# The last feed-forward part of two tiles held back, joined to 256 tokens and placed in the last tile's chain

## The chip, the core and the metric

The kernel runs on one core of one Trainium2 chip. A core has five instruction queues that run side by side: PE (TensorE, matmuls into PSUM; its weight loads are listed as PEld), DVE (VectorE), ACT (ScalarE), POOL (GpSimd) and SP (SyncE, which here issues nearly all DMAs). The metric is the device time of one execution in microseconds (us), as the median of several runs. One further execution was taken by the hardware profiler, and all views quoted here are of that one.

## The reference

Three layers are applied to 16 sequences of 64 tokens, 1024 tokens of 256 numbers in all. Each layer is added to its input after a layer norm.

```python
x = x + xattn(layernorm(x), ctx_2048, ...)   # self- and cross-attention, 16 heads over 1601 context rows per sequence
x = x + attn(layernorm(x), ...)              # block attention and a gated feed-forward with ternary weights
x = x + ffn(layernorm(x), ...)               # the part that this change moves

def ffn(x, gate_w, up_w, down_w, gate_s, up_s, down_s):
    g = einsum('th,ih->ti', x, gate_w) * gate_s      # 256 -> 704
    u = einsum('th,ih->ti', x, up_w) * up_s          # 256 -> 704
    return einsum('ti,hi->th', silu(g) * u, down_w) * down_s   # 704 -> 256
```

Nearly all work is in the cross-attention of the first layer. Everything is in float32 or rounded to coarser grids inside it.

## The kernel before

The 1024 tokens are eight tiles of 128 tokens (two sequences each). The tiles are counted from 0 in the code (`i`), so the sixth, seventh and last tile are `i` = 5, 6 and 7.

**Units.** For each tile there are two halves of the heads (`hh`) and two sequences (`bb`), so four units, and each unit goes through 13 chunks of up to 128 context rows (`unit`, L465). A chunk is projected to keys (L488, `ps_k`), squared and normalised (L493 to L507), transposed (L521, `tr_kx`), scored (L534, `s`), and 18 to 20 steps later, when the maximum over all chunks is known, exponentiated (L585 on DVE, L589 on ACT) and summed with the context rows into three PSUM accumulators (L604, `acc`). The context rows for the last step are loaded by L481 into five rotating buffers `ctxN`.

**After a unit.** The sums are divided (L613 to L618, `pq`), transposed (`turn_contexts`, L627, `tr_pc`) and, once per half, multiplied by the value weights and the output weights (`pair_out`, L647: `po_x` at L661, rounding on DVE at L673 and L192 to L265, `po_p` at L278, added to the tile's row `xr[i]` at L282). For the last half of the last tile `gap` is `None`, and both groups are done without a pause between them.

**Last parts.** `last_parts` (L782) then does layers two and three for one tile of 128 tokens. It is one long chain: a norm, the quantised projection (L774 transposes `tr_aq`, L792 `ps_qk`, L797 `ps_v`), the rotation (`r1`, `r2`), the transposes `tr_qk` (L821), four quarters of small attention, the output projection `po_o` (L885, added at L886), a norm ending in `hn` (L752), `tr_hn` (L893), the first feed-forward (L900 `ps_g`, `ps_u`; L909 `po_d`), and then the part that the change moves: the norm `xn3`, its transpose (L922), six chunks of 128 or 96 inner features (L938, four matmuls into `pgu`; Silu on ACT at L943; the product on DVE at L944), and `po_f` (L956, six matmuls), scaled and added on DVE (L961, L962) and stored (L963).

**What sets the order.** Every piece of work is a generator with a step and a rank on a heap (`spawn`, `at`, `run`, L83 to L100): a lower step goes first, then a lower rank, and `yield n` puts the rest n steps later. A tile takes 52 steps. `last_parts` of tile `i` starts at step 52*i + 92; for the seventh tile at +80 and for the last at +74 (L997). A scheduling layer below that then moves instructions of an engine past each other when the program is built, with the written order as priority, and puts in all waits. After that each engine's order is fixed.

**Buffers.** Weights for all of this come by DMA into one pool `wp` of ten buffers (L65, `piece` at L200). The DMAs stand in SP's queue in a fixed order, and one that waits for a buffer holds those behind it. `s_tile` and `tr_tile` take one of three PSUM banks, `ps_mm` has two more, used for `ps_k`. The pool `pp` (19 buffers) holds the exponentiated chunks.

The lines that the steps below use:

```python
        l0 = base + {NT - 2: 80, NT - 1: 74}.get(i, 92)
        spawn(l0, 2.5, last_parts(i, l0))
```

Of the kernel before, what the change touches and what calls it, by code (L numbers as in the profile page):

```python
# [14 lines left out]
F32 = mybir.dt.float32  # L15
# [8 lines left out]
P = 128  # L24
# [34 lines left out]
def body(tc, ctx, a):  # L59
# [586 lines left out]

    def pair_out(i, hh, gap):  # L647
# [28 lines left out]
        if gap is None:  # L676
            ws = [w_p, weights("wproj", 5 + 2 * hh)]
            pos = [group(gp) for gp in range(2)]
            for gp in range(2):
                project_out(i, rounded(gp, pos[gp]), ws[gp])  # L680
            return
# [56 lines left out]
    def b2(name):  # L738
        return one.tile([P, 512], F32, tag="b2", name=name, bufs=3)
# [42 lines left out]
    def last_parts(i, start):  # L782
# [3 lines left out]
        norm_apply(xa, xr[i], st, 1, H)  # L786
        h = yield from rmsnorm(xa, rows[:, 0, :], "h")
# [16 lines left out]
        q4 = qk.rearrange("p (h e d) -> p h e d", h=32, e=2)  # L804
        r1, r2 = b2("r1"), b2("r2")
# [80 lines left out]
        V.scalar_tensor_tensor(xa, po[:, 0:H], f, xa, ALU.mult, ALU.add)  # L886
        w_up = [piece("wup", (lambda t: t, cols_of("ffn_up_w", 0, 1024)[:, k, :])) for k in range(2)]
# [20 lines left out]
        for k in range(4):  # L908
# [18 lines left out]
        for c, (c0, n) in enumerate(CHUNKS):  # L927
            if c == 3:
                w_gu = [
                    piece("w_ff", (lambda t: v2(t[:, 0:640]), cols_of(name, 384, 320))) for name in ("gate_w", "up_w")  # L930
                ]
                yield 2
            c1 = c0 if c < 3 else c0 - 384
            pgu = s_tile("pgu")
            for e in range(2):
                w = v2(w_gu[e][:, 0 : 768 if c < 3 else 640])
                for k in range(2):
                    PE.matmul(  # L938
                        pgu[:n, e * P : (e + 1) * P], lhsT=w[:, k, c1 : c1 + n], rhs=xT[:, k, :],
                        start=k == 0, stop=k == 1,  # L940
                    )
            sgc = one.tile([P, P], F32, tag="sgc", name="sgc", bufs=2)
            A.activation(sgc[:n], pgu[:n, 0:P], AF.Silu, scale=col("gate_s", c)[:n])  # L943
            V.scalar_tensor_tensor(hd[:n, c, :], pgu[:n, P : 2 * P], col("up_s", c)[:n], sgc[:n], ALU.mult, ALU.mult)  # L944
            yield 1
        w_dn = [
# [5 lines left out]
        yield 2  # L952
        po = s_tile("po_f")
        for c, (c0, n) in enumerate(CHUNKS):
            w = w_dn[c // 4]
            PE.matmul(  # L956
                po[:, 0:H], lhsT=hd[:n, c, :], rhs=w[:n, (c % 4) * H : (c % 4 + 1) * H],
                start=c == 0, stop=c == len(CHUNKS) - 1,
            )
# [3 lines left out]
        nc.sync.dma_start(out=outs[i], in_=ot)  # L963

# [19 lines left out]
    for i in range(NT):  # L984
# [12 lines left out]
        l0 = base + {NT - 2: 80, NT - 1: 74}.get(i, 92)  # L997
# [4 lines left out]
    for n, (kind, p) in enumerate(order):  # L1002
        spawn(10 + 11 * n // 5, 5.8, split(kind, p))
    run()
# [71 lines left out]
```

## Time and profile before

| what | value |
|---|---|
| median of 3 runs | 2736.43 us (2736.36 to 2739.67) |
| time of the profiled execution | 2737.68 us |
| its span, first to last instruction | 2735.9 us |
| mean granted TensorE clock | 0.984 |
| PE, DVE, ACT, POOL busy | 95%, 69%, 52%, 31% |
| instructions | 41767 |
| `pgu` matmuls of one tile (L938) | 48 |
| `po_f` matmuls of one tile (L956) | 12 |

A float32 matmul of the program appears as two matmul instructions in the records, so four matmuls of a chunk are 8 instructions, and the six of `po_f` are 12. The mean duration of a matmul includes the latency of its pipeline; what one costs in a row of them is read from the chain of waits, where pieces follow one another without overlap. The last unit's accumulation ends at about 2653 us of the span, and from there to the end there is only the last tile's chain, with PE partly idle. In the timeline a bracket at the end of a row gives the idle time of the engine before it, and what ended it.

### The profile page before, as it was taken

Reading aid. Unit: us, or ns where it says so; the run is one execution under the profiler, and the core shown is the slowest. Engines: PE = TensorE matmul, PEld = TensorE weight load, DVE = VectorE, ACT = ScalarE, POOL = GpSimd, SP = SyncE. Lnnn points to the kernel's source line nnn. Section 1 sums busy time; section 2 is a strip of 40 time slices with the busy share of each in tenths; the row PEclk is TensorE's granted clock in tenths of the full one; section 3 lists DMA queues with packets and bytes.
Section 4 is the critical chain, followed back from the end, with each engine's and each line's share of the span. In section 5 each row is a group of like instructions: output and inputs, shape, how many; then the busy total and the mean of one; then the engine's idle time right before and its main releaser. Section 6 shows DMA issues by size and latency. Waiting matters only on the chain.

```text
span 2735.9 us, 41767 instructions
## 1 busy us (share of the span) xinstructions
PE 2611.4 (95%) x14875; PEld 2020.9 (74%) x14883; DVE 1894.5 (69%) x4643; ACT 1426.7 (52%) x2590; POOL 849.7 (31%) x1248
## 2 busy tenths in 40 slices
PE   6999989999999999999999999999999999999995
PEld 4677767768777787777877777776877778777773
DVE  7777766767667676677766676676766767666654
ACT  4555545445565555645457445564456545565431
POOL 3433323332333323333233333323333233333200
PEclk9999999999999999999999999999999999999996
DMA  7555734333344333434334344433434433343140
GB/s 256 190 176 196 236 124 139 102 105 122 115 144 144 118 92 117 153 121 125 109 118 143 111 127 126 130 125 99 140 109 145 129 110 117 120 138 101 46 124 20
DMA packets 215560, 353.09 MB, mean 129 GB/s; under 512 B 27164, under 2 KB 156088, under 8 KB 215352
## 3 DMA queue, kind: packets, MB, share of 16 engines
q1 hardware_dynamic: 215064, 350.25, 40.5%
q8 instruction: 118, 1.93, 0.3%
q14 instruction: 90, 0.74, 0.1%
q10 hardware_dynamic: 288, 0.17, 0.0%
HBM read 327.47 MB, written 22.87 MB: 128 GB/s over the span
## 4 chain that ended last, share of the span: by engine, by line
PE 71%; DVE 17%; POOL 6%; ACT 4%; issue 2%; DMA 1%; SPq 0%; ACTq 0%; POOLq 0%; DVEq 0%
PE ps_k L488 21%; PE acc L604 20%; PE s L534 10%; PE tr_kx L521 5%; POOL rs L160 2%; DVE ss L499 2%; PE po_p L278 2%; DVE P L585 2%; DVE M L544 2%; DVE kn L507 2%; PE po_x L661 2%; PE ps_q L324 1%; POOL rsx L160 1%; PE pgu L938 1%; POOL ve L159 1%
## 5 line engine op out<-in xcount | busy, mean ns | idle before, releaser
L604 PEld LDWEIGHTS acc<-ctxN,P 128*128 128x128 f32 (+1 forms) x4160 | 709.4, 191 | 175.1 <-issue 106.7
L488 PE MATMUL ps_k<-wkx,ctxT 128*128 128x512 f32 (+1 forms) x1664 | 801.9, 603 | 7.7 <-DVE wkx L973 7.3
L604 PE MATMUL acc<-ctxN,P 128*128 128x257 f32 (+5 forms) x4160 | 800.9, 340 | 0.0
L159 POOL TENSOR_SCALAR ve<-ss 128x4 f32<-128x4 f32 (+2 forms) x432 | 214.1, 496 | 1467.4 <-DVE ss L499 1383.3
L589 ACT ACTIVATE P<-P 128x512 f32<-128x512 f32 (+1 forms) x416 | 261.2, 630 | 519.5 <-DVE P L585 518.4
L534 PE MATMUL s<-qx,kT 128*128 128x128 f32 (+1 forms) x3328 | 445.3, 277 | 21.7 <-ACT kT L523 9.1
L160 POOL TENSOR_TENSOR rsx<-ve,nhalf 128x4 f32<-128x4 f32 (+1 forms) x416 | 440.5, 1059 | 31.6
L534 PEld LDWEIGHTS s<-qx,kT 128*128 128x128 f32 (+1 forms) x3328 | 406.0, 188 | 42.5 <-ACT kT L523 13.6
L488 PEld LDWEIGHTS ps_k<-wkx,ctxT 128*128 128x128 f32 (+1 forms) x1664 | 283.4, 190 | 206.1 <-issue 194.5
L544 DVE TENSOR_TENSOR M<-s,M 128x512 f32<-128x512 f32 (+1 forms) x384 | 263.6, 687 | 236.2 <-ACT P L539 234.0
L493 ACT ACTIVATE sq<-ps_k 128x512 f32<-128x512 f32 (+1 forms) x416 | 248.4, 597 | 331.4 <-PE ps_k L488 325.3
L499 DVE TENSOR_REDUCE ss<-sq 128x4 f32<-128x512 f32 (+1 forms) x416 | 283.3, 681 | 136.6 <-ACT sq L493 134.6
L539 ACT ACTIVATE P<-s 128x512 f32<-128x512 f32 (+1 forms) x416 | 246.8, 593 | 160.3 <-PE s L534 158.1
L523 ACT ACTIVATE kT<-tr_kx,vec 128x512 f32<-128x512 f32 (+1 forms) x416 | 315.9, 759 | 27.5 <-PE tr_kx L521 27.5
L507 DVE TENSOR_TENSOR kn<-ps_k,rsx 128x512 f32<-128x512 f32 (+1 forms) x416 | 283.0, 681 | 13.9 <-POOL rsx L160 13.7
L585 DVE TENSOR_TENSOR P<-P,mx 128x512 f32<-128x512 f32 (+1 forms) x416 | 282.2, 681 | 0.0
L521 PE MATMUL tr_kx<-ident,kn 128*128 128x128 f32 (+1 forms) x1664 | 246.9, 271 | 22.4 <-DVE kn L507 14.1
L521 PEld LDWEIGHTS tr_kx<-ident,kn 128*128 128x128 f32 (+1 forms) x1664 | 192.3, 142 | 36.5 <-DVE kn L507 12.8
L178 DVE TENSOR_SCALAR qn<-qn,mv,rs 128x128 f32<-128x128 f32 x256 | 76.2, 342 | 83.1 <-POOL rs L172 83.0
L160 POOL TENSOR_TENSOR rs<-ve,nhalf 128x4 f32<-128x4 f32 (+2 forms) x144 | 113.8, 790 | 8.3
L168 DVE BATCH_NORM_STATS2 st<-qn 128x6 f32<-128x128 f32 x256 | 63.8, 272 | 37.4 <-ACT qn L334 37.4
L278 PE MATMUL po_p<-wproj,cat 128*128 128x256 f32 x512 | 84.7, 309 | 3.8 <-DVE cat L265 3.7
(193 smaller groups left out, 2596.9 us busy)
## 6 DMA issues: line engine op xcount, KB each, us to landing
wproj<-wproj SPq DMA_DIRECT2D x120, 512.0 KB
ctxT<-in_ctx SPq DMA_DIRECT2D x192, 256.0 KB
ctxN<-in_ctx_n SPq DMA_DIRECT2D x384, 128.0 KB
wq<-wq SPq DMA_DIRECT2D x56, 512.0 KB
wkv<-wkv SPq DMA_DIRECT2D x56, 512.0 KB
wqx<-wqx SPq DMA_DIRECT2D x56, 512.0 KB
wvx<-in_w_kv_x SPq DMA_DIRECT2D x16, 512.0 KB
wup<-in_ffn_up_w SPq DMA_DIRECT2D x16, 512.0 KB
```

Source lines behind the costliest of these rows:

```text
L160: GP.tensor_tensor(out, ve[:n, :g], nhalf[:n, :g], ALU.pow)
L488: PE.matmul(ps[:n, :], lhsT=st["cxT"][c // 2][:, k, o : o + n], rhs=wkx[:, k, 512 * hh : 512 * (hh + 1)], start=k == 0, stop=k == 1,)
L493: A.activation(sq[:n], ps[:n], AF.Square)
L499: mark["ss"] = V.reduce_sum(ss[:n], st["ss"].pop(c)[:n].rearrange("p (g d) -> p g d", g=4), axis=AX.X)
L507: mark["kn"] = V.tensor_tensor(kn[:n].rearrange("p (g d) -> p g d", g=4), ps[:n].rearrange("p (g d) -> p g d", g=4), rs[:n].unsqueeze(2).t ...
L521: PE.transpose(tr[:, g * P : g * P + n], kn[:n, g * D : (g + 1) * D], ident[:n, :n])
L523: A.activation(kT[:, :, 0:n], tr.rearrange("p (g t) -> p g t", g=4)[:, :, 0:n], AF.Identity, bias=col("kxln_b"), scale=col("kxln_w"),)
L534: PE.matmul(ps[:n, g * P : (g + 1) * P], lhsT=kT[:, g, 0:n], rhs=qxs[i, hh][:, bb, 2 * g : 2 * g + 2, :].rearrange("p h s -> p (h s)"), st ...
L544: mark["M"] = V.tensor_tensor(st["M"][:n], ps[:n], st["M"][:n], ALU.max)
L585: ins = V.tensor_tensor(pc[:n], pc[:n], st["mx"][:n].rearrange("p g q -> p (g q)"), ALU.subtract)
L589: A.activation(pc[:n], pc[:n], AF.Exp)
L604: PE.matmul(ps, lhsT=pc[:n, g * P : (g + 1) * P], rhs=cx[:n, o : o + w], start=g == 2 and c == 0, stop=c == NC - 1 and (g, o) in ((2, 0), ...
```

## The change

The last feed-forward part of tiles 5 and 6 (`LATE`) no longer runs where `last_parts` of these tiles ends. There the normalised and transposed rows are only copied into one buffer of 256 tokens (`xT_late`), and the function returns. The work is split into eight functions in the list `late`: six chunks (`late_chunk`, on 256 tokens at once) and two `late_down` (one for each tile, on 128 tokens). The last tile's chain calls them with `fill(n)`: three in `pair_out` between `po_x` and the rounding, three behind the first norm in `last_parts`, one before the rotation, and one behind the addition of `po_o`. Their weights are asked for at step 430 (`late_weights`), those of the second three chunks with chunk 0. The chunks take their PSUM from `ps_mm` and their results from `pp`. The start of the sixth tile's `last_parts` is moved from +92 to +96. The code of a chunk and of the down projection becomes functions of their own (`gate_weights`, `gated`, `down_weights`, `down`), which the other tiles use as before.

```diff
+    late = []
+    def fill(n):
+        for fn in late[:n]:
+            fn()
+        del late[:n]
...
             pos = [group(gp) for gp in range(2)]
+            fill(3)
             for gp in range(2):
                 project_out(i, rounded(gp, pos[gp]), ws[gp])
...
         norm_apply(xa, xr[i], st, 1, H)
+        if i == NT - 1:
+            fill(3)
         h = yield from rmsnorm(xa, rows[:, 0, :], "h")
...
         q4 = qk.rearrange("p (h e d) -> p h e d", h=32, e=2)
+        if i == NT - 1:
+            fill(1)
...
         V.scalar_tensor_tensor(xa, po[:, 0:H], f, xa, ALU.mult, ALU.add)
+        if i == NT - 1:
+            fill(1)
...
-        w_gu = [
-            piece("w_ff", (lambda t: v2(t[:, 0:768]), cols_of(name, 0, 384))) for name in ("gate_w", "up_w")
-        ]
+        w_gu = gate_weights(0) if i not in LATE else None
...
             PE.transpose(tr[:, k * P : (k + 1) * P], xn[:, k * P : (k + 1) * P], ident)
+        if i in LATE:
+            V.tensor_copy(
+                xT_late()[:, :, (i - LATE[0]) * P : (i - LATE[0] + 1) * P],
+                tr[:, 0:256].rearrange("p (k t) -> p k t", k=2),
+            )
+            return
...
+    def gated(c, w_gu, xT, hd, sg):
+        (c0, n), m = CHUNKS[c], xT.shape[2]
+        c1, w = (c0, 768) if c < 3 else (c0 - 384, 640)
+        pgu = s_tile("pgu") if m == P else ps_mm.tile([P, 512], F32, tag="mm", name="pgu_late")
+        for e in range(2):
+            for k in range(2):
+                PE.matmul(
+                    pgu[:n, e * m : (e + 1) * m], lhsT=v2(w_gu[e][:, 0:w])[:, k, c1 : c1 + n], rhs=xT[:, k, :],
+                    start=k == 0, stop=k == 1,
+                )
+        A.activation(sg[:n], pgu[:n, 0:m], AF.Silu, scale=col("gate_s", c)[:n])
+        V.scalar_tensor_tensor(hd[:n], pgu[:n, m : 2 * m], col("up_s", c)[:n], sg[:n], ALU.mult, ALU.mult)
...
+    def down(i, hd, w_dn):
         po = s_tile("po_f")
...
+    LATE = [NT - 3, NT - 2]
+    held = {}
+    def xT_late():
+        if "xT" not in held:
+            held["xT"] = qp.tile([P, 512], F32, tag="qn", name="xT_late").rearrange("p (k t) -> p k t", k=2)
+        return held["xT"]
+    def late_weights():
+        held["gu"], held["dn"] = gate_weights(0), down_weights()
+    def late_chunk(c):
+        m = 2 * P
+        if c == 0:
+            held["gu2"] = gate_weights(1)
+        if c % 2 == 0:
+            held[c] = pp.tile([P, 512], F32, tag="P", name="hd_late")
+        sg = pp.tile([P, 512], F32, tag="P", name="sg_late")[:, 0:m]
+        o = (c % 2) * m
+        gated(c, held["gu" if c < 3 else "gu2"], held["xT"], held[c - c % 2][:, o : o + m], sg)
+    def late_down(j):
+        o = j * P
+        hd = [held[c - c % 2][:, (c % 2) * 2 * P + o : (c % 2) * 2 * P + o + P] for c in range(6)]
+        down(LATE[j], hd, held["dn"])
+    for c in range(6):
+        late.append(lambda c=c: late_chunk(c))
+    for j in range(2):
+        late.append(lambda j=j: late_down(j))
...
-        l0 = base + {NT - 2: 80, NT - 1: 74}.get(i, 92)
+        l0 = base + {NT - 3: 96, NT - 2: 80, NT - 1: 74}.get(i, 92)
...
+    at(52 * (NT - 1) + 66, 0, late_weights)
     run()
```

More of the change, by code (lines that the diff above doesn't have):

```diff
@@ L926, in last_parts, with gate_weights, down_weights @@
         hd = one.tile([P, 768], F32, tag="t3", name="hd3").rearrange("p (c t) -> p c t", c=6)
-        for c, (c0, n) in enumerate(CHUNKS):
+        for c in range(6):
             if c == 3:
-                w_gu = [
-                    piece("w_ff", (lambda t: v2(t[:, 0:640]), cols_of(name, 384, 320))) for name in ("gate_w", "up_w")
-                ]
+                w_gu = gate_weights(1)
                 yield 2
[L933 to L941, printed above, removed]
             sgc = one.tile([P, P], F32, tag="sgc", name="sgc", bufs=2)
-            A.activation(sgc[:n], pgu[:n, 0:P], AF.Silu, scale=col("gate_s", c)[:n])
-            V.scalar_tensor_tensor(hd[:n, c, :], pgu[:n, P : 2 * P], col("up_s", c)[:n], sgc[:n], ALU.mult, ALU.mult)
+            gated(c, w_gu, xT, hd[:, c, :], sgc)
             yield 1
-        w_dn = [
+        w_dn = down_weights()
+        yield 2
+        down(i, [hd[:, c, :] for c in range(6)], w_dn)
+    def gate_weights(e):
+        o, n = (0, 384) if e == 0 else (384, 320)
+        return [piece("w_ff", (lambda t: v2(t[:, 0 : 2 * n]), cols_of(name, o, n))) for name in ("gate_w", "up_w")]
+    def gated(c, w_gu, xT, hd, sg):
[10 more added lines that the diff above has]
+        V.scalar_tensor_tensor(hd[:n], pgu[:n, m : 2 * m], col("up_s", c)[:n], sg[:n], ALU.mult, ALU.mult)
+    def down_weights():
+        return [
             piece("w_dn", (lambda t: t.rearrange("p (c o) -> p c o", c=4),
@@ L951, in last_parts @@
         ]
-        yield 2
+    def down(i, hd, w_dn):
         po = s_tile("po_f")
         for c, (c0, n) in enumerate(CHUNKS):
-            w = w_dn[c // 4]
             PE.matmul(
-                po[:, 0:H], lhsT=hd[:n, c, :], rhs=w[:n, (c % 4) * H : (c % 4 + 1) * H],
+                po[:, 0:H], lhsT=hd[c][:n], rhs=w_dn[c // 4][:n, (c % 4) * H : (c % 4 + 1) * H],
                 start=c == 0, stop=c == len(CHUNKS) - 1,
@@ L963, in last_parts @@
         nc.sync.dma_start(out=outs[i], in_=ot)
+    LATE = [NT - 3, NT - 2]
[19 more added lines that the diff above has]
+        down(LATE[j], hd, held["dn"])
+    for c in range(6):
+        late.append(lambda c=c: late_chunk(c))
+    for j in range(2):
+        late.append(lambda j=j: late_down(j))
     def centre(hh):
```

## The prediction

> **What bounds the kernel now.** I read the page first, then the busy time by stages, then the chain of waits from 2630 us on, then PE's timeline behind it. The page says that PE is busy nearly all the time and that only the last of 40 slices is different, in PE's share and in the clock granted to it:
>
> ```profile
> PE 2611.4 (95%) x14875; PEld 2020.9 (74%) x14883; DVE 1894.5 (69%) x4643; ACT 1426.7 (52%) x2590; POOL 849.7 (31%) x1248
> ...
> PE   6999989999999999999999999999999999999995
> ...
> PEclk9999999999999999999999999999999999999996
> ```
>
> The table by stages (each row: stretch; its length; busy us of PE, PEld, DVE, ACT, POOL; clock; DMA share; GB/s) covers the sixth tile's chunks, the seventh tile's chunks and parts of the last chain:
>
> ```profile
> 2430.00:2493.00 63.00, 61.47 (x368) 48.53 (x368) 45.16 (x103) 45.44 (x77) 20.05 (x29) 1.00 0.43 132
> ...
> 2632.00:2653.00 21.00, 21.00 (x140) 19.57 (x139) 2.10 (x6) 2.20 (x6) 0.00 (x0) 1.00 0.33 102
> 2653.00:2665.74 12.74, 8.96 (x49) 7.49 (x47) 8.18 (x25) 1.91 (x4) 0.00 (x0) 1.00 0.38 110
> 2665.74:2686.22 20.48, 8.20 (x33) 6.49 (x34) 9.92 (x24) 3.43 (x6) 3.02 (x5) 0.50 0.26 85
> ...
> 2696.46:2710.12 13.66, 7.51 (x17) 3.54 (x17) 4.04 (x15) 2.39 (x4) 0.74 (x2) 0.50 0.00 0
> ...
> 2713.53:2727.18 13.65, 8.11 (x37) 6.84 (x38) 4.74 (x12) 0.99 (x3) 0.79 (x2) 0.50 0.00 1
> ```
>
> Where the removed work stands now, PE has no pause worth the name (61.47 of 63 us, 21.00 of 21). In the last chain it works 8.20 of 20.48 us, and most of that at half clock. The chain of waits (start, us, what) gives the prices:
>
> ```profile
> 2632.56 0.89 PE pgu L938 x8
> 2633.45 1.75 PE acc L604 x10
> ...
> 2655.38 2.59 PE po_f L956 x12
> 2657.98 1.74 PE po_x L661 x8
> ...
> 2721.40 8.33 PE pgu L938 x48
> ```
>
> Between 2630.8 and 2653.2 the chain is PE alone, accumulations with chunks of the seventh tile between them. A chunk on 128 tokens is 0.87 to 0.89. Eight passes of 256 columns (`po_x`) are 1.74: a chunk on 256 tokens will cost as much as two on 128. PE's work is not made less, only moved. The pauses, in PE's timeline (idle time in the brackets), are where it goes:
>
> ```profile
> 2663.27 1.22 PE L278 MATMUL po_p<-wproj,cat 128*128 128x256 f32 x8 [1.84 <-DVE cat L265]
> 2666.21 2.05 PE L278 MATMUL po_p<-wproj,cat 128*128 128x256 f32 x8 [1.72 <-DVE cat L265]
> 2674.96 0.40 PE L774 MATMUL tr_aq<-identb,aq_q 128*128 128x128 bf16 x2 [6.70 <-DVE aq_q L768]
> ...
> 2680.30 1.09 PE L821 MATMUL tr_qk<-ident,r 128*128 128x128 f32 x4 [3.10 <-DVE r L817]
> ...
> 2704.01 0.66 PE L893 MATMUL tr_hn<-ident,hn 128*128 128x128 f32 x2 [2.64 <-DVE hn L752]
> ```
>
> **What the Trainium skill says.** "TensorE: Matmul & The Clock Gate", Part 1, has the half clock: an idle window of some 3.4 us halves it, a busy one restores it. The trace agrees: 0.50 begins at 2665.74, behind a window with 1.2 us of matmuls in 3.4, and lasts in multiples of 3.41. The same page, "Architectural detail", says that ACT and DVE are strict FIFO; all I say of queues below rests on that and on the order in the built program. "ScalarE: Activation LUTs", "What ACT_TABLE_LOAD costs", has about 1283 ns for a load; the group of these loads has the same 1283 ns here.
>
> **The change, part by part.** All times are against the profiled execution (2737.68, of which 2735.9 span; its median neighbours are at 2736.43, 1.25 lower, so I subtract the same gain from 2736.43).
>
> 1. *Sixth tile.* Removed: six chunks of 0.88 and `po_f` of 2.59, 7.87 us of PE. PE is busy 97.6% there, so I take 7.5 (bounds 6.3 and 7.9).
>
> 2. *Around it.* Each of its Silus sat between exponentials on ACT, so 12 table loads of 1.28 go, and one PE wait of 0.9 for `hd` (L944) that they caused. The start at +96 takes the first norm and quantisation (some 2.8 us of DVE: `xa`, `h`, `am`, `aq_u`, `aq_q`) from a place where PE stands still for them:
>
> ```profile
> PE tr_m L551 <- ACT qx L343: 2.5, 1, 2.5
> ```
>
> In the built order this work comes later, between the rounding of a self-attention group, where it will hold something else. I take 1.0 for all of this (bounds a loss of 1.5, a gain of 3.4).
>
> 3. *Seventh tile.* Six chunks: 6 x 0.88 = 5.28 of a stretch that is PE alone. What would be late next? The exponentials end at 2625.6 (ACT's timeline), so not they. The context loads wait for the buffer five accumulations back and have 4 x 1.75 = 7 us. Two loads at the end of the chain (320 and 512 KB, issued 2668.07 and 2668.53) are over by 2672. I take 5.25 (4.5 to 5.3). `po_f` (2.59) goes too, but belongs to step 4. One set of six weight loads goes as well; SP's queue is not the bound.
>
> 4. *From the last accumulation (2653.0) to the second `po_p`.* The built order has half of chunk 0 before `tr_pc` (in the 0.69 us wait for `pq`), half behind it, then `po_x`, chunks 1 and 2, `po_p`, chunk 3, `po_p`, chunks 4 and 5. `po_x` no longer waits for `po_f`, only for ACT's two copies (over at 2656.4): it starts 1.55 earlier. Chunks 1 and 2 then end at 2663.35. But DVE now has the product of chunk 0 between the first halves of the rounding, and those of chunks 1 to 3 before the additions, 0.50 each (256 columns; by L886, 0.48). In DVE's order: first `q_y` 2658.35, `cat` 2663.4, first `po_p` 2663.95 to 2665.0, chunk 3 to 2666.75, second `po_p` to 2667.7 (full clock, against 2.05 at half), its addition at 2667.95 instead of 2668.29. So -0.35 (bounds -0.8 and +1.5). `w_ff` of chunk 3 is issued when `po_x` ends (2660); a load of its size took under 3 us, so it is there before 2665. The qkv weights stand behind it in SP's queue and wait for chunk 2: issued at 2663, needed at 2675. ACT's table load for the first Silu (1.28) stands behind the copies for `po_x` and hides beside `po_x`; without that cover it would cost its 1.28.
>
> 5. *To `tr_aq`.* Chunks 4 and 5 run in the 6.70 us pause. The product of chunk 4 hides in the wait for POOL; that of chunk 5 stands between `fsc` and `asc` on DVE: +0.5 (0 to 0.5).
>
> 6. *First `late_down`*, between `ps_v` and `tr_qk`: 12 passes of 0.216 at full clock, 5.2 at half, in a pause of 3.3. PE has then been nearly idle for 6 us, so I take half clock until a full busy window is over, about 4.3 us in: it ends 1.5 late. With the clock up, `tr_qk` (1.09) takes 0.66 and the first scores (2.09 at half) take 0.89: -1.6. Taken: +0.2 (-0.4 to +1.9). That busy window is spent earlier than before, so a part of `tr_p` and `av` may meet half clock: +0.3.
>
> 7. *Second `late_down`*, between `po_o` and `tr_hn`. Here DVE's order is what counts: the scaling and addition of its output (0.42 each) stand **ahead of `hn`** and wait for its last matmul. `hn`, the transposes and the whole feed-forward are queued behind. Start 2701.2, some 4.8 us mostly at half clock, 0.2 latency, 0.84 of DVE: `hn` at 2707.05 instead of 2703.38, +3.67. The clock then saves 0.3 at `tr_hn` and about 1.0 of the 6.14 us of `ps_g` and `ps_u`. Taken: +2.4 (+1.0 to +3.9). On SP the last tile's `w_dn` now waits behind the store of the first output (about 2683) and is needed at 2729: nothing.
>
> 8. *The last tile's own chunks* (8.33, of which 5.8 at half clock, when 3.4 to 6.8 are possible): -0.3 on average (-1 to +0.5).
>
> Cost of the tail: -0.35 + 0.5 + 0.2 + 0.3 + 2.4 - 0.3 = 2.75. Sum: -7.5 - 1.0 - 5.25 + 2.75 = **-11.0**, so 2726.7 for a profiled execution and **2725.4** for the median.
>
> **The rivals.**
>
> *A, as worked out:* 2725.4, own range 2721.5 to 2729.5. Chance 0.70.
>
> *B, the tail takes back more.* Both `late_down` wholly at half clock (+1.85, +3.9) and the rounding 2 us late behind chunk 3: 2.0 + 0.5 + 1.85 + 3.9 + 0.6 = 8.85 against 13.75, so -4.9: 2731.5. For it speaks that PE is nearly idle before both. Chance 0.11.
>
> *C, the moved work keeps the clock up.* Both `late_down` in 2.6 us: the first hides, the second costs 1.5, `ps_g` and `ps_u` save 2.7, the scores 1.6, the last chunks 2: -13.75 + 0.15 - 1.6 + 1.5 - 2.7 - 2 = -18.4: 2718. Against it: pauses of over 3.4 us remain. Chance 0.13.
>
> *D, slower: the clock is halved from `po_x` on.* Then a chunk costs 3.5: second addition +6.3, chunk 5's product holds `aq_u` (together +8.8), `late_down` +1.85 and +3.7, the last chunks and `po_f` wholly at half (15.6 against 10.94) +4.7: 19.0 against 13.75, +5.3: 2741.7. It decides from 13.75 us in the tail on. Against it: in the changed order PE has work without a gap of 1 us from 2653 to 2671. Chance 0.06.
>
> **How the numbers follow.** Under 0.2% (5.5 us) a measurement here cannot be told from no change. Faster (below 2731.0): A, C and a part of B, 0.86. Within: the rest of B and half of D, 0.10. Slower: 0.04. The range leaves out D, half of B and the lower half of C: 2720 to 2731.
>
> **What would show it.** Right: between 2632 and 2653 only accumulations, 1.75 apart; `po_x` 1.5 nearer to the last of them; the wait of `tr_m` gone near 2214; clock 1.00 to about 2670; `hn` waiting for the second `po_f` through `ot`. Wrong: PE waiting for `ctxN` or for `w_ff` in chunk 3; new waits of PE between 2240 and 2400; the second `late_down` over in 2.6 us; a tail, from the last accumulation to the end, more than 6 us longer than the 82.9 of before.

## The result, and the profile after

| kernel | median, us | runs | ratio to before (95% interval) |
|---|---|---|---|
| before | 2737.01 | 18 | |
| changed | 2731.24 | 18 | 0.9977 (0.9970 to 0.9984) |
| changed, measured again beside other runs | 2731.58 | 21 | 0.9977 (0.9970 to 0.9983) |

The change makes the kernel 0.23% faster, 5.8 us of the 11.0 that were forecast. The median lies 0.2 us above the forecast range; but the kernel before measured 0.6 us more here (2737.01) than the 2736.43 that the forecast started from, and counted as a difference the 5.8 us lie at the slow edge of the range (5.4 to 16.4 us faster). The profiled execution took 2729.80 us with a span of 2728.0: 7.9 us less than before.

On the page of the changed kernel, the busy time of PE and the slices that carried the argument read so:

```profile
PE 2616.5 (96%) x14835; PEld 2022.0 (74%) x14835; DVE 1892.1 (69%) x4637; ACT 1410.4 (52%) x2572; POOL 847.3 (31%) x1248
...
PE   6999989999999999999999999999999999999996
...
PEclk9999999999999999999999999999999999999997
```

PE has 40 matmul records fewer than before (x14835 against x14875). That alone says nothing, because two chunks on 128 tokens became one with as many matmuls of twice the columns. But the columns to be multiplied are as many as before, and PE has 5.1 us more busy time (2616.5 against 2611.4). So some of the matmuls met a slower clock; the slices are too coarse to show where.

To find the place I cut both traces at three events: the start of the fifth tile's `po_f` (up to there both kernels do the same), `tr_xn` of the seventh tile, and the last accumulation. Rows of the table by stages (stretch; length; busy us of PE, PEld, DVE, ACT, POOL; clock; DMA share; GB/s), first of before:

```profile
2162.66:2630.40 467.74, 458.67 (x2662) 359.58 (x2663) 323.89 (x758) 253.18 (x451) 137.67 (x198) 1.00 0.35 109
2630.40:2653.33 22.93, 22.93 (x150) 21.34 (x150) 2.66 (x8) 2.20 (x6) 0.00 (x0) 1.00 0.34 103
2653.33:2735.90 82.57, 46.67 (x228) 35.76 (x227) 39.29 (x103) 14.57 (x28) 4.55 (x9) 0.71 0.13 39
```

and of the changed kernel:

```profile
2161.47:2625.72 464.25, 454.34 (x2604) 353.67 (x2603) 320.72 (x750) 234.63 (x432) 137.33 (x198) 0.99 0.33 105
2625.72:2643.32 17.60, 17.60 (x101) 16.00 (x102) 0.55 (x2) 0.00 (x0) 0.00 (x0) 1.00 0.15 43
2643.32:2728.00 84.68, 60.13 (x289) 47.35 (x287) 42.24 (x111) 18.70 (x35) 4.55 (x9) 0.80 0.18 56
```

Stage B (the accumulations) lost 5.33 us, as forecast (5.25). Stage C (the last chain) grew by 2.1, near the 2.75 forecast. Stage A, which holds the sixth tile's part and its later start, lost only 3.49 where steps 1 and 2 together said 8.5. The 1.2 us ahead of stage A are the same instructions in both kernels, so they are not an effect of the change. The sum is -1.2 - 3.5 - 5.3 + 2.1 = -7.9.

PE's waits in stage A of the changed kernel (waiting instruction, who ended the wait: us in total, times, longest) show two that before did not have:

```profile
PE tr_kx L521 <- DVE q_y L444: 2.6, 1, 2.6
PE po_p L278 <- ACT qn L334: 1.9, 1, 1.9
...
PE tr_m L551 <- ACT qx L343: 0.3, 1, 0.3
```

The wait of `tr_m` is gone (2.5 before, 0.3 now), as step 2 said, but a wait of 2.6 for `q_y` has come at `tr_kx` (before, the longest wait at that place was 0.8) and one of 1.9 at `po_p`. DVE's timeline has the cause of the first (start, us, operation, in brackets its idle time and what ended it):

```profile
2225.91 0.68 DVE L507 TENSOR_TENSOR kn<-ps_k,rsx 128x512 f32<-128x512 f32 x1
...
2227.10 0.68 DVE L585 TENSOR_TENSOR P<-P,mx 128x512 f32<-128x512 f32 x1
2229.76 0.48 DVE L761 SCALAR_TENSOR_TENSOR h<-xa,rs,rows 128x256 f32<-128x256 f32 x1 [1.98 <-POOL rs L160]
...
2230.62 0.75 DVE L444 TENSOR_TENSOR q_y<-po_s,rsc 128x256 f32<-128x256 f32 x2
```

and POOL's timeline says what `rs` waited for:

```profile
2227.27 0.83 POOL L159 TENSOR_SCALAR ve<-ss 128x4 f32<-128x4 f32 x2 [3.48 <-DVE ss L499]
2228.18 1.03 POOL L160 TENSOR_TENSOR rsx<-ve,nhalf 128x4 f32<-128x4 f32 x1
2229.18 0.55 POOL L160 TENSOR_TENSOR rs<-ve,nhalf 128x1 f32<-128x1 f32 x1
```

DVE stands idle at `h` for 1.98 us, because POOL first waits for the sum of the next keys (`ss`) and computes their scale (`rsx`). Everything behind `h` on DVE waits too, and so does `q_y`. What `tr_kx` transposes, `kn`, was ready at 2226.6; it waits for a PSUM bank. `q_y` empties the two banks of `po_s`, and `tr_kx` takes one of the same three. In the kernel before, the same idle time stood ahead of the same `h`:

```profile
2210.51 0.48 DVE L752 SCALAR_TENSOR_TENSOR h<-xa,rs,rows 128x256 f32<-128x256 f32 x1 [1.97 <-POOL rs L160]
```

There the work behind it (`P` at 2214.64, then `qx` on ACT at 2215.89) ended in the wait of `tr_m`. So the wait of before had not gone; it had moved along with the part.

The clock is what the page could not show. Windows of 3.41 us around the two waits, changed kernel:

```profile
2227.62:2231.03 3.41, 0.91 (x8) 0.72 (x7) 1.39 (x5) 1.23 (x2) 1.95 (x4) 1.00 0.14 38
2231.03:2234.45 3.42, 3.36 (x7) 1.92 (x8) 3.24 (x12) 0.78 (x1) 0.00 (x0) 0.50 0.00 0
2258.34:2261.75 3.41, 1.46 (x13) 1.23 (x13) 3.31 (x9) 1.42 (x3) 1.38 (x2) 1.00 0.84 289
2261.75:2265.17 3.42, 3.42 (x11) 2.39 (x11) 2.82 (x12) 0.85 (x2) 0.37 (x2) 0.50 0.46 141
```

Each wait leaves PE less than half busy for a window (0.91 and 1.46 us), and in the next window, at half clock, it is busy throughout. Before, stage A had no such window.

The last chain, in PE's timeline of the changed kernel:

```profile
2625.97 17.63 PE L604 MATMUL acc<-ctxN,P 128*128 128x257 f32 x100
...
2655.64 1.30 PE L278 MATMUL po_p<-wproj,cat 128*128 128x256 f32 x8
...
2664.02 0.28 PE L783 MATMUL tr_aq<-identb,aq_q 128*128 128x128 bf16 x2 [3.63 <-DVE aq_q L777]
...
2690.15 0.61 PE L898 MATMUL po_o<-tern_w,aq_t 128*128 128x256 bf16 x2 [0.39 <-DVE aq_t L785]
2690.55 5.08 PE L986 MATMUL po_f<-w_dn,hd_late 128*128 128x256 f32 x12
2697.09 0.41 PE L908 MATMUL tr_hn<-ident,hn 128*128 128x128 f32 x2 [1.46 <-DVE hn L761]
```

Only accumulations stand between `tr_xn` and the chain (100 in a row), and the wait of 6.70 at `tr_aq` is filled down to 3.63. From `po_o` to `tr_hn` it is now 6.94 us where it was 3.24.

### The profile page after: what moved, and what is told of

It reads as the page before. It is cut to its first block, busy times and chain, and to the rows that moved or that the text cites. A ratio compares the mean times of both kernels' runs of the same rounds, so it can differ in the third digit from the quotient of the medians.

```text
span 2728.0 us, 41628 instructions
## 1 busy us (share of the span) xinstructions
PE 2616.5 (96%) x14835; PEld 2022.0 (74%) x14835; DVE 1892.1 (69%) x4637; ACT 1410.4 (52%) x2572; POOL 847.3 (31%) x1248
## 4 chain that ended last, share of the span: by engine, by line
PE 71%; DVE 17%; POOL 6%; ACT 4%; issue 2%; DMA 1%; SPq 0%; ACTq 0%; POOLq 0%; DVEq 0%
PE ps_k L488 21%; PE acc L604 20%; PE s L534 10%; PE tr_kx L521 5%; DVE ss L499 2%; POOL rs L160 2%; PE po_p L278 2%; DVE P L585 2%; DVE M L544 2%; DVE kn L507 2%; PE po_x L669 2%; POOL rsx L160 1%; PE ps_q L324 1%; POOL ve L159 1%; DVE st L168 1%
## 5 line engine op out<-in xcount | busy, mean ns | idle before, releaser
L159 POOL TENSOR_SCALAR ve<-mv,wsq 128x4 f32<-128x4 f32 (+1 forms) x96 | 28.8, 300 | 186.6 <-DVE mv L169 177.6
```

The costliest lines, as they stand in the source:

```text
L159: GP.tensor_scalar(ve[:n, :g], in_, scale, EPS, ALU.mult, ALU.add)
```

## The experiments

Theory 1: the later start (+96) of the sixth tile's part is what failed, by the moved wait and by the clock behind it. Theory 2: the start does not matter, and the sixth tile's part was worth less than 7.5. Each run stood beside runs of the kernel before on the same chip, and the ratio is to these. The chips differ, so the medians of different rows can be compared only where the column "before beside it" is the same; the changed kernel itself was run only beside 2737.01 and 2738.11. The stages are cut like those above.

| run | median, us | before beside it | ratio (95%) | A | PE busy in A | half-clock windows in A (at its end) | C |
|---|---|---|---|---|---|---|---|
| before | 2737.01 |  |  | 467.74 | 458.67 | 0 | 82.57 |
| changed | 2731.24 | 2737.01 | 0.9977 (0.9970, 0.9984) | 464.25 | 454.34 | 2 (0) | 84.68 |
| changed, again | 2731.58 | 2738.11 | 0.9977 (0.9970, 0.9983) | 467.41 | 457.40 | 4 (2) | 80.51 |
| changed, start +92 | 2726.59 | 2739.68 | 0.9956 (0.9943, 0.9968) | 461.77 | 452.64 | 1 (0) | 84.93 |
| before, start +96 | 2742.48 | 2739.68 | 1.0010 (1.0004, 1.0017) | 471.23 | 462.04 | 2 (1) | 83.41 |
| part from `h` on a step later | 2726.43 | 2739.68 | 0.9956 (0.9943, 0.9969) | 464.16 | 455.61 | 3 (2) | 82.78 |
| second `late_down` moved | 2727.02 | 2739.68 | 0.9952 (0.9940, 0.9964) | 464.29 | 454.29 | 2 (0) | 81.09 |
| `h` without `rs` | 2730.29 | 2738.11 | 0.9967 (0.9955, 0.9978) | 460.39 | 451.38 | 0 | 85.00 |
| no held-back work | 2727.62 | 2738.11 | 0.9967 (0.9954, 0.9980) | 464.27 | 454.24 | 2 (0) | 81.38 |
| start +92, `late_down` moved | 2728.87 | 2738.11 | 0.9964 (0.9952, 0.9977) | 460.44 | 451.30 | 0 | 81.34 |
| scale from the variance, `late_down` moved | 2728.45 | 2737.60 | 0.9967 (0.9957, 0.9977) | 467.12 | 455.93 | 3 (2) | 81.06 |
| the same, start +92 | 2728.97 | 2737.60 | 0.9974 (0.9964, 0.9984) | 468.17 | 457.14 | 4 (1) | 80.88 |
| part a step later, `late_down` moved | 2721.20 | 2737.60 | 0.9949 (0.9936, 0.9961) | 464.10 | 455.64 | 3 (2) | 80.31 |
| seventh tile alone held back | 2729.86 | 2737.07 | 0.9979 (0.9969, 0.9989) | 467.79 | 458.79 | 0 | 80.70 |

The medians and ratios are of several runs, the other columns of each kernel's one trace (us). A half-clock window is a stretch of 3.41 us for which the record has a granted clock of 0.50; the record changes the clock only in multiples of this length. The end of A is the stretch from the seventh tile's `ps_g` to `tr_xn`, which no edit touches. It takes 16.7 us in the eight traces that have no half clock there and 18.2 to 19.8 us in the other six. All of them have the same wait of 1.3 us in it, at `tr_pc`. What an edit did to A is therefore read from A without its end: 451.07 us before, 447.6 to 447.7 in all four traces with the changed kernel's order.

**The changed kernel again.**

> The changed kernel as it is, for comparison on the same chip as the runs beside it. If its pauses near 2231 and 2262 belong to the order and not to chance, the 2.6 and the 1.9 us are there again at the same places; the windows at half clock behind them may or may not be, and the time spreads over some 4 us with them. Ratio to the kernel before between 0.997 and 0.9985 as measured first.

The ratio is the same. The waits of 2.6 and 2.0 stand at the same places, each with its window at half clock, and two more such windows stand at 2621 to 2628, at the end of A, where the first trace had none. Stage A is 3.16 longer for these two, and the tail is 4.2 shorter than in the first trace, with the same instructions in the same order. Single traces of this kernel are thus read by busy time and waits, not by their length alone.

**The start back at +92.**

```diff
-        l0 = base + {NT - 3: 96, NT - 2: 80, NT - 1: 74}.get(i, 92)
+        l0 = base + {NT - 2: 80, NT - 1: 74}.get(i, 92)
```

> The changed kernel with the sixth tile's last part started at +92 again, nothing else. Theory 1, the shift is what failed: at +96 PE meets two new pauses (2.6 us behind h, 1.9 us behind the rope products) and two windows at half clock (about 1.7 us each), 7.9 us together; at +92 the pause of tr_m (2.5) comes back. So it is 3 to 5.5 us faster than the changed kernel: about 2727 (2725.5 to 2728.5), and the time from the start to tr_xn of the seventh tile falls by as much. Theory 2, the start does not matter and the sixth tile's own part was oversized (PE had more hidden idle time than I took): 2731 within 1 us. Theory 3, the start at +96 is needed (at +92 the exponentials or the seventh tile's part collide): slower than 2732.

2726.59 us, in the range of theory 1. By the ratios that is 5.7 us below the changed kernel, a little more than the 3 to 5.5 expected. In the trace stage A fell by 2.5, to 461.77, although one window at half clock stood in it, behind the returned wait of `tr_m`:

```profile
2210.77:2214.18 3.41, 1.16 (x8) 0.97 (x8) 2.84 (x8) 1.01 (x2) 1.47 (x2) 1.00 0.06 20
2214.18:2217.59 3.41, 3.07 (x7) 1.92 (x8) 1.91 (x6) 1.96 (x10) 0.11 (x1) 0.50 0.00 0
```

**The kernel before with the start at +96 alone.** The same edit, the other way round, in the kernel before.

> The kernel before with the start of the sixth tile's last part at +96 and nothing else. Theory 1: the tr_m pause (2.5) goes and pauses of 2.6 and 1.9 with their half clock come: 2.5 to 5 us slower than before, about 2740.5. Theory 2 (the shift alone costs nothing): 2737 within 1 us. As the prediction had it (the shift is worth 0 to 1): 2736 to 2737.

Slower than before by 0.10% (interval 0.04% to 0.17%), 2.8 us. The waits are those of the changed kernel, with none of its other parts present:

```profile
PE tr_kx L521 <- DVE q_y L444: 2.6, 1, 2.6
...
PE po_p L278 <- ACT qn L334: 1.9, 1, 1.9
```

Time not busy hardly changed (9.19 us in stage A, 9.07 before); busy time rose by 3.4, in two windows at half clock. One of these two stands behind the wait of 2.6; the other, at 2626.5, stands at the end of A, and the wait of 1.9 has none behind it. Without the end, A is 453.02 against 451.07, 1.95 us longer. So the shift is shown to cost time, and both waits belong to it; how many windows at half clock follow differs from trace to trace.

**The part from `h` on a step later.**

```diff
-    def rmsnorm(src, wrow, name):
+    def rmsnorm(src, wrow, name, n=1):
...
-        yield 1
+        yield n
...
-        h = yield from rmsnorm(xa, rows[:, 0, :], "h")
+        h = yield from rmsnorm(xa, rows[:, 0, :], "h", 2 if i == NT - 3 else 1)
```

> The changed kernel, but in the sixth tile h (and all of that part behind it) is issued one step later, so that the scale rs from POOL is there when DVE reaches h. Theory 1a, the pause is DVE standing behind h for POOL's rs (1.98 us in DVE's timeline): the pause of 2.6 at tr_kx near 2231 and its window at half clock go, 3 to 4.5 us faster than the changed kernel, 2727 to 2728, unless the rope products find a new victim (then 2729). Theory 1b, the pause is DVE's sheer work of 2.8 us, as the prediction had it: the pause stays or moves one step on, 2731 within 1.5.

The time is below the 2727 to 2728 of theory 1a (2726.43; by the ratios 5.7 us below the changed kernel), but not for its reason. The scheduling layer left `h` where it was on DVE, ahead of `q_y`, and the wait of 2.6 stayed. What moved was the work behind it: the rope products came a step later, the wait of 1.9 at `po_p` was gone, and a wait of 1.6 at `tr_kx` stood elsewhere. Stage A is 464.16 with three windows at half clock, but two of these stand at its end, as in the second trace of the changed kernel. Without the end, A is 444.4 against 447.6, 3.2 us shorter: the wait at `po_p` and its window are gone. For the first wait the run is inconclusive. It does show that the second one hangs on the rope products. In the changed kernel's timelines of DVE

```profile
2256.53 1.30 DVE L178 TENSOR_SCALAR qn<-qn,mv,rs 128x128 f32<-128x128 f32 x1
...
2259.61 0.68 DVE L585 TENSOR_TENSOR P<-P,mx 128x512 f32<-128x512 f32 x1
```

and of ACT

```profile
2260.33 0.63 ACT L589 ACTIVATE P<-P 128x512 f32<-128x512 f32 x1 [3.81 <-DVE P L585]
2260.86 0.57 ACT L334 COPY qn<-ps_q 128x512 f32<-128x512 f32 x1
```

the chain is read so: while POOL works on its product (L819, 2256.23 to 2257.74), a scaling that takes 0.34 just before takes 1.30 on DVE; `P` is late; ACT's exponential stands in front of the copy that `po_p` waits for. This chain was not tried apart.

**`h` without the wait for `rs`.** In the sixth tile (`free`) `h` is left unscaled: a constant stands in the place of `rs`. The scheduling layer then puts `h` right behind `xa`; DVE has the same work.

```diff
-        V.scalar_tensor_tensor(h, src, rs, wrow, ALU.mult, ALU.mult)
+        V.scalar_tensor_tensor(h, src, nhalf[:, 0:1] if free else rs, wrow, ALU.mult, ALU.mult)
...
-        h = yield from rmsnorm(xa, rows[:, 0, :], "h")
+        h = yield from rmsnorm(xa, rows[:, 0, :], "h", i == NT - 3)
```

> The changed kernel, but h of the sixth tile takes a constant in the place of the scale rs, so it does not wait for POOL (rs is still computed and not used; the sixth tile's h is left unscaled, so its output is another). The work of DVE is the same. Theory 1a, the pause of 2.6 at tr_kx is DVE standing at h for POOL's rs: the pause falls under 0.6 us and the window at half clock behind it goes; 2.5 to 4.5 us faster than the changed kernel. Theory 1b, as the prediction had it, the pause comes from the 2.8 us of DVE's own work: a pause of 2 us or more stays somewhere between 2215 and 2240, and the time is within 1 us of the changed kernel.

```profile
PE po_p L278 <- ACT qn L334: 2.0, 1, 2.0
...
PE tr_kx L521 <- DVE q_y L444: 1.0, 1, 1.0
```

The wait fell from 2.6 to 1.0, not under 0.6, and no window of stage A ran at half clock: 460.39 us, 3.9 less than the changed kernel's first trace. That is theory 1a for the cause of the first wait; the 1.0 that remains is put down to DVE's own work, which was not tried apart. Not all of the 3.9 belongs to the edit: the wait of 2.0 at `po_p` is still there and only happens to have no window at half clock behind it. The runs as a whole gained less (2730.29, 1.3 us below the changed kernel beside it, with overlapping intervals): the tail of this trace is 85.0 and its first 2166 us are 4.8 longer than in the first trace of the changed kernel, with the same instructions.

**The second `late_down` moved.**

```diff
         V.scalar_tensor_tensor(xa, po[:, 0:H], f, xa, ALU.mult, ALU.add)
-        if i == NT - 1:
-            fill(1)
...
-    def act_quant(src, w, j):
+    def act_quant(src, w, j, also=lambda: None):
...
         V.tensor_scalar(f, am, wmean[:, j : j + 1], 1.0 / 127.0, ALU.mult, ALU.mult)
+        also()
         yield 1
...
-        sT, f = yield from act_quant(sg, 512, 2)
+        sT, f = yield from act_quant(sg, 512, 2, (lambda: fill(1)) if i == NT - 1 else (lambda: None))
```

> The changed kernel with the second late_down moved from between po_o and tr_hn to the last quantisation of the last tile's chain (on DVE behind fsc, on PE ahead of tr_aq). Theory of step 7, the scaling and addition ahead of hn hold the whole chain: tr_hn comes 3.6 us sooner after po_o (3.3 instead of 6.9), ps_g and ps_u take back 0.5, the moved product hides in the pause before tr_aq but for 0 to 0.8: 2.3 to 3.1 us faster than the changed kernel, 2728 to 2729. Rival, it only changes its place: at half clock it holds tr_aq by 1.5 to 2.5 us and the gain is under 1 us: 2730.5 to 2731.

DVE of the changed kernel at the old place:

```profile
2690.80 0.48 DVE L899 SCALAR_TENSOR_TENSOR xa<-po_o,fsc,xa 128x256 f32<-128x256 f32 x1 [0.70 <-PE po_o L898]
2695.67 0.42 DVE L991 TENSOR_TENSOR ot<-po_f,rows 128x256 f32<-128x256 f32 x1 [4.39 <-PE po_f L986]
...
2696.47 0.48 DVE L761 SCALAR_TENSOR_TENSOR hn<-xa,rs,rows 128x256 f32<-128x256 f32 x1
```

PE of the kernel with the move:

```profile
2690.95 0.61 PE L899 MATMUL po_o<-tern_w,aq_t 128*128 128x256 bf16 x2 [0.39 <-DVE aq_t L786]
2694.20 0.66 PE L907 MATMUL tr_hn<-ident,hn 128*128 128x128 f32 x2 [2.64 <-DVE hn L761]
...
2700.94 2.76 PE L985 MATMUL po_f<-w_dn,hd_late 128*128 128x256 f32 x12
2704.70 0.40 PE L784 MATMUL tr_aq<-identb,aq_q 128*128 128x128 bf16 x4 [1.00 <-DVE aq_q L777]
```

`ot` made DVE wait 4.39 us with `hn` behind it. Moved, `tr_hn` comes 3.25 after `po_o` instead of 6.94, 3.7 sooner, and `late_down` hides at full clock in front of `tr_aq`, which still waits for DVE. The tail is 81.09; in five traces with this order it is 80.3 to 81.3 (mean 80.9), in five with the changed kernel's order 80.5 to 85.0 (mean 83.6). The ratio is 0.9952 against 0.9977; the intervals do not overlap. That difference, 6.8 us, is more than the tail gives (2.7) and more than was expected (2.3 to 3.1). The two ratios were taken on different chips, and what lies beyond the tail is not explained.

**No held-back work at all.** The eight late functions do nothing but store the two tiles' rows, and the weights for them are not loaded.

```diff
     for c in range(6):
-        late.append(lambda c=c: late_chunk(c))
+        late.append(lambda: None)
     for j in range(2):
-        late.append(lambda j=j: late_down(j))
+        late.append(lambda j=j: bare(j))
...
-    at(52 * (NT - 1) + 66, 0, late_weights)
```

> The changed kernel without the held-back work: the six chunks on 256 tokens and both late_down are left out, the outputs of the sixth and seventh tile are stored without that part. It gives the price of that work in the last chain. By the prediction's terms the time from the last accumulation to the end falls by the two chunk halves ahead of po_x (0.9 each), 0.5 of chunk 5's product, 0.5 around the first late_down and 2.4 to 3.2 of the second, less what more windows at half clock give back (po_p, ps_g, scores: 1 to 2): 3.5 us shorter (2.5 to 5). If the held-back work keeps the clock up so that it pays for itself: less than 1.5 us shorter. If it costs much more than I took: over 6 us.

The tail is 81.38, 3.3 below the first trace of the changed kernel and 2.2 below its mean; the median is 4.0 us lower. The forecast of 3.5 holds within what the tail itself varies. With the second `late_down` moved, the tail with all of the held-back work (80.9) is no longer than this one without it: on balance the six chunks and the first `late_down` cost the chain nothing. Without them PE is nearly idle and more of the chain runs at half clock (mean clock 0.73 against 0.80).

**Both edits together.**

> The changed kernel with both edits that stand alone in two runs before: the sixth tile's start at +92 and the second late_down in the last quantisation. They touch places 300 us apart, so the gains should add: 3.9 (trace) and 2.5 to 3.6, together 6 to 7.5 us faster than the changed kernel, ratio to the kernel before 0.9932 to 0.9942. If they do not add (the clock windows take one back): 4 us, 0.995.

In the trace they add: stage A 460.44 and tail 81.34, the sum of both gains, and no window at half clock in stage A. In the times they do not: 2728.87 in five runs (2724.62 to 2730.96), 2.7 us below the changed kernel on the same chip, where 6 to 7.5 had been expected, and the intervals of the two ratios overlap. The part ahead of stage A, the same in all kernels but the two with the scale from the variance, takes between 2160.0 and 2166.3 us in these traces, and five runs do not resolve the rest. So the sizes of the two single gains rest on the traces.

**The scale of `h` from the variance, in all tiles.** The second `late_down` stands in its new place here too.

```diff
-        h = yield from rmsnorm(xa, rows[:, 0, :], "h")
...
+        GP.tensor_tensor(ss, st[1][:, 0:1], st[1][:, 0:1], ALU.mult)
+        GP.tensor_tensor(ss, ss, st[0][:, 0, 1:2], ALU.mult)
...
+        rsqrt(rs, ss, 1.0, 1)
+        yield 1
...
+        V.scalar_tensor_tensor(h, xa, rs, rows[:, 0, :], ALU.mult, ALU.mult)
```

> The changed kernel with the second late_down in the last quantisation and, in all eight tiles, the scale of h worked out on POOL from the variance that is there already (rs squared times the variance), so that ACT's square and its sum go and POOL's rs no longer queues behind the sum of a later key. Five earlier tiles show the same pause as the kernel before at 2214 (tr_m waiting, 2.1 to 2.5 us each, DVE standing at h). If the wait for rs is the cause, the tr_m pauses fall by 1.5 to 2.5 us in each of five tiles and the 2.6 near 2231 to about 1, and less half clock follows them: 10 to 16 us faster than the run of the second late_down moved alone, ratio to the kernel before about 0.990. If the pauses come from DVE's own work, or the three POOL operations more hold the keys' scale instead: within 3 us of it, 0.994 to 0.996.

> The same with the sixth tile's start at +92. With the wait for rs gone there as well, neither the 2.5 of tr_m nor the 2.6 and 1.9 of the later start remain: 1 to 4 us faster than with +96, ratio about 0.989. If the start is of no account once the waits are gone: equal within 1.5 us.

Both missed the gain that was expected: 2728.45 (ratio 0.9967, 0.9957 to 0.9977) and, with +92, 2728.97 (0.9974, 0.9964 to 0.9984). The five earlier waits of `tr_m` stayed at 2.5 each. The scheduling layer still put the last two POOL operations behind the keys' `ve`, so the queue was the same; POOL of the run with the start at +96, in the fifth tile:

```profile
1876.33 0.83 POOL L159 TENSOR_SCALAR ve<-ss 128x4 f32<-128x4 f32 x2 [1.79 <-DVE ss L499]
1877.25 1.02 POOL L160 TENSOR_TENSOR rsx<-ve,nhalf 128x4 f32<-128x4 f32 x1
1878.23 0.55 POOL L160 TENSOR_TENSOR rs<-ve,nhalf 128x1 f32<-128x1 f32 x1
```

`h` waited 1.97 us for that `rs`, as before. So the runs say nothing on what the waits are worth in the earlier tiles. In stage A a new wait of 2.7 came at `tr_r`, and the time not busy rose to 11.2 and 11.0 us, from 10.0 and 9.1 in the same kernels without this edit.

**The part a step later and `late_down` moved.**

> The changed kernel with both edits that stand alone in two runs before: the sixth tile's part one step later from h on (which there moved the rope products, and with them the pause of 1.9 at po_p, not h) and the second late_down in the last quantisation. If the gains add: 4 to 7 us faster than the changed kernel, ratio 0.9935 to 0.995. If only the tail's edit is real: 2.5 to 3.5, 0.995 to 0.996.

2721.20 us in five runs (2718.84 to 2725.81), ratio 0.9949 (0.9936 to 0.9961): faster than both kernels, and the lowest median of all versions; its interval overlaps those of the versions with one of the edits. In the trace the gains add: its tail is 80.31, and its stage A, 464.10, again has two of its three windows at half clock at the end. Without the end it is 444.4, 3.2 below the changed kernel's.

**The seventh tile's part alone held back.**

```diff
-    LATE = [NT - 3, NT - 2]
+    LATE = [NT - 2]
...
-        m = 2 * P
+        m = P
...
-    for j in range(2):
-        late.append(lambda j=j: late_down(j))
+    late.append(lambda: late_down(0))
...
-        l0 = base + {NT - 3: 96, NT - 2: 80, NT - 1: 74}.get(i, 92)
+        l0 = base + {NT - 2: 80, NT - 1: 74}.get(i, 92)
```

> Only the seventh tile's part is held back: the sixth tile works and starts as in the kernel before (+92), the six late chunks have 128 tokens, there is one late_down (in the place of the first) and none ahead of hn. By the steps: the stage up to tr_xn of the seventh tile is that of before, the stage of the accumulations loses its 5.3 us, and the last chain keeps only the cheap part of the held-back work and no late_down ahead of hn, so it is 0 to 3 us shorter than before. Together 5.5 to 8 us faster than before, ratio 0.997 to 0.998: as fast as the whole change, which means that the sixth tile's part (7.3 us of PE) is paid back by the half clock at its start and by the second late_down. If the sixth tile's part brings something net, this run is slower than the whole change by 2 us or more: 2733 to 2735, ratio above 0.9983.

2729.86 us, as fast as the whole change within the intervals. Its stages:

```profile
2160.00:2627.79 467.79, 458.79 (x2664) 359.36 (x2663) 323.81 (x758) 251.88 (x450) 137.87 (x198) 1.00 0.35 110
2627.79:2645.40 17.61, 17.60 (x101) 16.01 (x102) 0.55 (x2) 0.00 (x0) 0.00 (x0) 1.00 0.14 44
2645.40:2726.10 80.70, 51.20 (x277) 40.83 (x275) 40.69 (x109) 17.94 (x35) 4.56 (x9) 0.80 0.18 57
```

Stage A is that of before to 0.05 us, stage B loses 5.3, and the tail is 1.9 shorter than before. Half of the change gives, within the intervals, all of its gain: by the traces, the sixth tile's 7.4 us of PE are paid back by its later start (up to 3.8) and by the second `late_down` (about 3).

## Why the prediction held in direction and missed in size

**Where it held.** The direction and the mechanism: rival A, less of it. Step 1 said -7.5: with the start at +92 and no half clock, PE's busy time in stage A is 451.30 against 458.67, -7.4, with the time not busy unchanged (9.14 and 9.07). Step 3 said -5.25 and nothing late next: -5.3 in every trace in which the part is held back, and no wait for `ctxN` or `w_ff`.

**Where it failed: step 2, "Around it", taken as a gain of 1.0 with bounds from a loss of 1.5 to a gain of 3.4.** It came out as a loss of 3.8 (464.25 against 460.44 with +92), outside the bounds. With one window at half clock in the trace of +92 the loss is 2.5, and in the kernel before with the start at +96, without the end of A, 1.95: each time beyond the bound. The step saw 2.8 us of DVE work leave the place where `tr_m` waited, and supposed that only this work would hold something elsewhere. Two things were left out. The work begins with an idle wait of 2 us for POOL, which stood in DVE's timeline ahead of `h` and moved with it; the run without the wait for `rs` took the new wait of PE from 2.6 to 1.0. And the step priced a pause of PE at its own length. In time not busy the shift costs only 0.8 us (9.91 against 9.14), inside the bounds; the other 3.0 are busy time, two windows at half clock behind the two waits. In both traces of the changed kernel these two windows are there, and in the two other traces with the same order of that stage. The prediction had looked for half clock in the tail alone: "clock 1.00 to about 2670" was among its own signs, and so were "new waits of PE between 2240 and 2400" (they came at 2231 and 2261). The other gains of the step brought nothing either: at +92 the 12 table loads and the wait of 0.9 for `hd` are gone, but waits of 0.7 at `tr_r` and 0.3 at `po_p` have come, and the time not busy is that of before.

Between the two first traces the forecast of -11.0 and the measured -7.9 differ by 3.1: +4.8 from step 2, -0.6 from the tail, -1.2 from ahead of stage A, where nothing was changed, and about 0.1 from steps 1 and 3.

**The tail.** Forecast +2.75, measured +2.1 in the first trace. By its steps, in time from the last accumulation: the addition behind the second `po_p` is 1.3 sooner, where step 4 had -0.35 and a bound of -0.8. The way on to `tr_aq` is 0.4 longer (step 5: +0.5), and up to `po_o` another 0.3 (step 6: +0.5). From `po_o` to the last tile's chunks it is 2.7 longer (step 7: +2.4), of which `tr_hn` alone is 3.7 later (+3.67 said). Step 8 brought nothing. So step 7, the largest, was right in mechanism and size; that the sum came out near is partly luck, since the size is not fixed to a microsecond. The second trace of the same kernel has a tail of 80.51, 2.1 shorter than before, because the second `late_down`, `ps_g` and the last chunks happened to meet more full clock (4.07, 1.98 and 6.95 us against 5.08, 3.19 and 8.26). Over five traces the mean is 83.6 against 83.0 for the two with before's tail, +0.6. The prediction gave bounds for single pieces of half clock, but took one phase of the clock for all runs.

**Rivals.** D (the clock halved from `po_x` on) did not happen: chunks on 256 tokens ran at 1.73 us for each, at full clock, up to 2660. C (the moved work keeps the clock up) happened in part: against the chain without any held-back work, the clock in the tail is 0.80 to 0.85 instead of 0.73, and the six chunks cost nothing on balance.

**Open.** The four runs beside the kernel before of 2739.68 lack the changed kernel. By the ratios, the versions with one edit among them are 5.7 to 6.8 us faster than it, while their traces show gains of 2.5 to 3.2 in the stage that was edited; the surplus is not explained. That the half clock alone, with the waits left in, costs the 3 us was not tried apart; it is read from traces of the same order with more and with fewer such windows.

## What to carry to other kernels

When a piece of work is moved, look at what its first instructions wait for in the trace, not only at how long they work: the idle time ahead of the piece goes with it and hits what stands behind it in the new place. A pause of 1.3 to 2.6 us on a busy TensorE was followed by none, one or two windows at half clock here, each some 1.5 us on top of the pause's own length. And when work is put into pauses of a chain, place the instruction that empties its result (here DVE's scaling) behind the chain's own next step; here that was worth 2.7 us in the means of five traces each, while the matmuls themselves were free on balance.

## What the hardware showed that I had not expected

The clock fell here long before PE was idle for a whole window. The Trainium skill ("TensorE: Matmul & The Clock Gate", Part 1) has the window of 3413 ns and says that it is free-running; it lists half clock after an idle window. Here windows with 0.91, 1.16 and 1.46 us of matmuls were followed by 3.41 us at half clock, and the window ahead of 2665.74, which the prediction took as agreeing, had 1.2 us of them too. The wait of 2.5 us at `tr_m`, behind which one trace with the start at +92 has half clock, has none in the other (start +92, `late_down` moved), where a border splits it between two windows:

```profile
2213.45:2216.86 3.41, 2.38 (x20) 2.05 (x18) 3.31 (x11) 0.00 (x0) 0.17 (x1) 1.00 0.12 38
2216.86:2220.27 3.41, 1.69 (x7) 1.07 (x8) 1.83 (x7) 2.97 (x11) 1.41 (x2) 1.00 0.00 0
```

But PE's busy time in a window, as the profile has it, does not decide it alone. In the changed kernel's second trace a window with 2.13 us was followed by two at half clock, while the kernel before with the start at +96 has one with 1.54 us (2261.29 to 2264.70) with full clock behind it:

```profile
2617.61:2621.03 3.42, 2.13 (x13) 1.72 (x11) 3.42 (x14) 3.41 (x7) 0.00 (x0) 1.00 0.67 239
2621.03:2624.44 3.41, 3.38 (x12) 1.96 (x12) 1.87 (x6) 1.68 (x4) 0.00 (x0) 0.50 0.06 20
```

Where the bound lies, and what is counted, these traces do not show. One half-clock window costs some 1.5 us of busy time (busy time in stage A over that of the trace with the start at +92 and no such window: 1.34 for one, 3.04 for two, 4.31 for three, 6.10 for four). With it, the place of the windows makes the same instructions take 464.3 or 467.4 us in stage A of the changed kernel, 461.8 or 460.4 with the start at +92, and 84.7 or 80.5 in the tail. The spread between runs fits this: of the changed kernel's 39 runs, those with a mean granted clock of 0.986 took 2727.1 to 2729.9 us, and those with 0.984 or less 2730.9 to 2737.0.
